# A two-layer GraphSAGE kernel: node aggregates kept in SBUF instead of a table of scanned rows in DRAM

## The chip, the cores and the metric

The kernel runs on one core of a Trainium2 chip. The metric is the device time of one execution in microseconds (us); smaller is better. Engines are named as in the profile: PE is TensorE (PEld its weight loads), DVE is VectorE, ACT is ScalarE, POOL is GpSimd, SP is SyncE, which here only issues DMAs.

## What is computed

12500 nodes with 128 features, 200000 edges (`src`, `dst`, a weight each), sorted by `dst`. Cut to what matters:

```python
h0   = relu(layernorm(x))
w    = edge_weight / max(segment_sum(edge_weight, dst), EPS)[dst]
feat = relu(h0 @ W_pool + b_pool)
neigh = segment_max(feat[src] * w[:, None], dst)        # 0 for a node without edges
rst  = h0 @ W1_self + neigh @ W1_neigh + b1
h    = relu(rst / max(norm(rst, axis=1), EPS))
neigh2 = segment_sum(h[src] * w[:, None], dst) / max(deg, 1)[:, None]
out  = x + relu(h @ W2_self + neigh2 @ W2_neigh + b2)
```

Each layer needs one row of 512 bytes for each edge, picked by `src`: 200000 rows gathered from a table in DRAM, twice.

## The kernel before

Nodes are cut into 98 tiles of 128, edges into 391 groups of 512 (390 whole ones, and one of 320). A group has four chunks of 128 edges. The program has five stages that follow each other, since each needs a table that the one before it leaves in DRAM.

**Prologue.** SP loads x (L114). For each node tile DVE works out mean and variance (L118, L119) and the normalized rows (L129); PE transposes them (L131), ACT takes the relu into `hT` (L132). PE multiplies with W_pool (L135) and adds the bias by a second matmul with one row (L136); DVE takes the relu `fr` (L138); SP stores it to the table `feat_d` (L139). Then the edge lists are loaded (L158 to L174), one group to a partition, and turned by PE transposes (L201) and DVE copies (L202) into columns: `srcT`, `ewT` and the high and low parts of `dst`. A number `unsorted`, worked out on the way, would send the kernel down a general path; with the inputs here it isn't taken.

**Edge phase**, once for each layer (`edge_phase`, L204). For each group POOL issues four indirect DMAs (L220), each of 128 rows of the table into `gt` (six buffers). ACT multiplies each chunk by the weights of its edges into `gs` (L225), PE transposes the chunks to `pm`, [feature, edge] (L227). PE spreads the row of segment starts over all partitions by a matmul with `pick` (L230), and ACT turns it into `keep` (L232). DVE runs one scan along the 512 edges (L235): a running max in layer 1, a running sum in layer 2, starting anew where `dst` changes, and carrying over from group to group. PE transposes the result back (`pr`, L243), ACT copies it to `rows` (L245), and SP stores the 256 KB to a table `scan_d` of 200000 rows (L246). In layer 1 DVE also makes one-hot tiles `a` and `b` (L254 to L259), from which PE sums each node's degree and weights (`hist`, L262).

**Node phase**, once for each layer. After layer 1's edges the degrees give the row of each node's last edge. For each four tiles POOL gathers those rows from `scan_d` (L305), DVE scales them (L309), PE transposes (L313), ACT copies (L315), and PE adds up the two products and the bias (L321 to L323). Layer 1 then divides by the norm (L365 to L372) and stores `h_d`, the second layer's table (L375); layer 2 adds x and stores the output (L396, L398).

The order on each engine is worked out by a scheduler from the program's order and its dependences; pools of buffers decide how far one engine may run ahead of another.

Of the kernel before, what the change touches and what calls it, by code (L numbers as in the profile page):

```python
# [16 lines left out]
P = 128  # L17
D = 128
G = 512          # edges of a group: one PSUM bank of fp32 columns
Q = 4            # chunks of 128 edges in a group; node tiles in a node group  # L20
NEG = -3.0e38    # below every message; added to the running maximum where a segment begins
LN_EPS = 1e-5
TINY = 1e-12     # EPS of the reference
PAST = 1 << 20   # a destination past every node, behind the last edge
SLOW_B = 64      # edges of one turn of the general path
# [3 lines left out]
def gnn_kernel(ctx, tc, x, src, dst, ew, w_pool, b_pool, w1s, w1n, b1, w2s, w2n, b2, out):  # L29
    """x + GraphSAGE(relu(layernorm(x))): a max-pooled layer and a mean layer over weighted edges.  # L30

    Edges are taken in order, in groups of 512. A group's source rows are gathered, weighted and
    transposed to [feature, edge]; one scan along the edges, restarted wherever dst changes, leaves
    each node's max (sum) at its last edge. The scanned rows go to a table in DRAM, and each node
    then fetches the row of its last edge. The edges come sorted by dst; a flag worked out on the
    chip says whether they are, and for edges in any other order a general path, one edge at a
    time, takes the scan's place.

    Node n = 128 * hi + lo lies on partition lo, column hi, of all per-node scalars.
    """  # L40
# [3 lines left out]
    HI = -(-N // P)                  # node tiles  # L44
    NP = HI * P                      # nodes, padded
    NF = N // P                      # whole node tiles
    GF, TAIL = divmod(E, G)          # whole groups, edges of the last one
    NG = GF + (TAIL > 0)
    NT = -(-NG // P)                 # blocks of 128 groups
    assert TAIL % Q == 0 and E % SLOW_B == 0 and E >= NP and D == x.shape[1]  # L50

    const = ctx.enter_context(tc.tile_pool(name="const", bufs=1))
    dram = ctx.enter_context(tc.tile_pool(name="dram", bufs=1, space=DRAM))
# [3 lines left out]
    scan1_d = dram.tile([E, D], F32, name="scan1_d")  # L57
    scan2_d = dram.tile([E, D], F32, name="scan2_d")

# [6 lines left out]
    for name, b in (("pool", b_pool), ("1", b1), ("2", b2)):  # L66
        Bv[name] = const.tile([1, D], F32, name=f"b_{name}")
        nc.scalar.dma_start(Bv[name], b[None, :])
    bp_col = const.tile([P, 1], F32)
    nc.scalar.dma_start(bp_col, b_pool[:, None])  # L70

    diff = const.tile([P, P], F32)      # column - partition
    nc.gpsimd.iota(diff, pattern=[[1, P]], base=0, channel_multiplier=-1,
                   allow_small_or_imprecise_dtypes=True)
    iota = const.tile([P, P], F32)      # column
    nc.gpsimd.iota(iota, pattern=[[1, P]], base=0, channel_multiplier=0,
                   allow_small_or_imprecise_dtypes=True)
    ident = const.tile([P, P], F32)
    nc.vector.tensor_scalar(ident, diff, 0.0, None, op0=OP.is_equal)
    upto = const.tile([P, P], F32)      # 1 where partition <= column  # L80
    nc.vector.tensor_scalar(upto, diff, 0.0, None, op0=OP.is_ge)
    ones = const.tile([P, P], F32)
    nc.vector.memset(ones, 1.0)

    hT = const.tile([P, HI, P], F32)    # layer inputs, [feature, node]
    begins = const.tile([P, NT, G], BF16)
    srcT = const.tile([P, NT, Q, P], I32)
    ewT = const.tile([P, NT, Q, P], F32)
    last = const.tile([P, HI], I32)     # row of each node's last edge
    s1 = const.tile([P, HI], F32)  # L90
    s2 = const.tile([P, HI], F32)
# [335 lines left out]
```

## Time and profile before

| | us |
|---|---|
| three runs of the kernel: median (lowest to highest) | 5526.82 (5515.38 to 5533.27) |
| span of the profiled execution, first to last instruction | 5500.3 |
| prologue, to the first gather of layer 1 | 0 to 262.8 |
| edge phase of layer 1 | 262.8 to 2703 |
| node phase of layer 1 | 2703 to 2944 |
| edge phase of layer 2 | 2944 to 5287 |
| node phase of layer 2 | 5287 to 5500 |

The profiled execution's own time isn't listed apart from its span; the median of the runs is 26.5 us above the span. A profile row such as `L220 POOL DMA_INDIRECT gt<-feat_d,srcT x1563 | 1564.4, 1001 | ...` gives the line of the program, the engine, the operation, what is written and read, how many there were, their busy time in us, the mean of one in ns, and then the engine's idle time just before them with what ended it. "issue" there means that the engine waited for nothing the profile could name. In a timeline row the first number is the start in us, the second the duration in us, and the idle time before stands in brackets. In a table of windows each engine's busy time stands with its number of instructions; behind them the granted TensorE clock (1 is full speed), the share of time in which DMA engines were busy, and GB/s.

### The profile page before, as it was taken

Reading aid. Unit: us, or ns where it says so; the run is one execution under the profiler, and the core shown is the slowest. Engines: PE = TensorE matmul, PEld = TensorE weight load, DVE = VectorE, ACT = ScalarE, POOL = GpSimd, SP = SyncE. Lnnn points to the kernel's source line nnn. Section 1 sums busy time; section 2 is a strip of 40 time slices with the busy share of each in tenths; the row PEclk is TensorE's granted clock in tenths of the full one; section 3 lists DMA queues with packets and bytes.
Section 4 is the critical chain, followed back from the end, with each engine's and each line's share of the span. In section 5 each row is a group of like instructions: output and inputs, shape, how many; then the busy total and the mean of one; then the engine's idle time right before and its main releaser. Section 6 shows DMA issues by size and latency. Waiting matters only on the chain. (4 is left out here: it accounts for less than half of the span.)

```text
span 5500.3 us, 41184 instructions
## 1 busy us (share of the span) xinstructions
PE 2928.3 (53%) x12192; PEld 2278.5 (41%) x12192; DVE 1829.8 (33%) x2502; ACT 1856.7 (34%) x4842; POOL 3234.2 (59%) x3328
## 2 busy tenths in 40 slices
PE   7645555565555555555585444444444444444459
PEld 4435554555545544555463223222222222222237
DVE  3334444444444444444422222222222222222211
ACT  0023333333333333333222333333333333333320
POOL 0066666666666666666444666666666666666653
PEclk9977777777777777777765555555555555555556
DMA  2122222222222222222221222223232222223233
GB/s 74 41 72 86 86 87 87 86 85 86 86 86 83 86 84 86 85 85 87 71 63 53 87 87 91 87 89 91 86 90 89 90 87 88 89 86 91 88 89 94
DMA packets 285584, 460.21 MB, mean 84 GB/s; under 512 B 67796, under 2 KB 131030, under 8 KB 285352
## 3 DMA queue, kind: packets, MB, share of 16 engines
q0 software_dynamic: 106304, 217.86, 15.4%
q1 hardware_dynamic: 178178, 239.30, 12.5%
q8 instruction: 100, 1.64, 0.1%
q14 instruction: 132, 1.08, 0.1%
q10 hardware_dynamic: 870, 0.33, 0.0%
HBM read 233.18 MB, written 224.05 MB: 83 GB/s over the span
## 5 line engine op out<-in xcount | busy, mean ns | idle before, releaser
L220 POOL DMA_INDIRECT gt<-feat_d,srcT x1563 | 1564.4, 1001 | 1105.8 <-issue 435.9
L220 POOL DMA_INDIRECT gt<-h_d,srcT x1563 | 1482.0, 948 | 905.4 <-issue 545.0
L235 DVE TENSOR_TENSOR_SCAN sc<-keep,sc,pm 128x512 f32<-128x512 f32 x780 | 997.3, 1279 | 2541.4 <-remote 1113.3
L243 PE MATMUL pr<-ident,sc 128*128 128x128 f32 x3128 | 786.5, 396 | 1557.5 <-DVE sc L235 977.6
L245 ACT ACTIVATE rows<-pr 128x512 f32<-128x512 f32 (+1 forms) x782 | 466.9, 597 | 2755.4 <-issue 2023.7
L243 PEld LDWEIGHTS pr<-ident,sc 128*128 128x128 f32 x3128 | 536.6, 216 | 1753.7 <-DVE sc L235 1065.4
L227 PE MATMUL pm<-ident,gs 128*128 128x128 f32 x3126 | 866.8, 372 | 346.4 <-ACT gs L225 240.0
L227 PEld LDWEIGHTS pm<-ident,gs 128*128 128x128 f32 x3126 | 574.5, 190 | 1113.5 <-ACT gs L225 519.4
L225 ACT ACTIVATE gs<-gt,ewT 128x128 f32<-128x128 f32 x3126 | 993.7, 393 | 118.1 <-DMA gt<-feat_d,srcT 75.0
L262 PE MATMUL hist<-a,b 128*128 128x196 f32 x3126 | 755.4, 397 | 0.0
L262 PEld LDWEIGHTS hist<-a,b 128*128 128x128 f32 x3126 | 708.9, 241 | 31.3 <-issue 0.2
L230 PE MATMUL pb<-begins,pick 128*128 128x512 bf16 (+1 forms) x782 | 419.8, 538 | 499.2 <-ACT rows L245 256.7
L232 ACT ACTIVATE keep<-pb 128x512 f32<-128x512 f32 (+1 forms) x782 | 462.4, 592 | 181.8 <-remote 139.3
L254 DVE TENSOR_TENSOR a<-hiT,iota 128x392 f32<-128x392 f32 x391 | 218.3, 558 | 558.8 <-remote 329.2
L305 POOL DMA_INDIRECT ng<-scan_d,last x196 | 187.1, 955 | 212.8 <-issue 52.7
L258 DVE TENSOR_TENSOR b<-loT,iota 128x512 f32<-128x512 f32 x391 | 268.9, 688 | 0.0
L256 DVE TENSOR_TENSOR a<-a,ewT 128x392 f32<-128x392 f32 x391 | 218.4, 558 | 0.0
L323 PE MATMUL po<-b,ones 1*128 1x128 f32 x392 | 130.6, 424 | 9.3 <-issue 9.3
L230 PEld LDWEIGHTS <-pick 128*128 128x128 bf16 x782 | 103.9, 133 | 16.4 <-issue 16.2
L315 ACT ACTIVATE nT<-pt 128x512 f32<-128x512 f32 (+1 forms) x50 | 28.7, 591 | 223.2 <-PE pt L313 164.8
L323 PEld LDWEIGHTS po<-b,ones 1*128 1x128 f32 x392 | 81.6, 257 | 45.4 <-issue 35.9
L135 PE MATMUL pf<-w_pool,hT 128*128 128x128 f32 x196 | 77.8, 501 | 9.0 <-ACT hT L132 9.0
(88 smaller groups left out, 1059.3 us busy)
## 6 DMA issues: line engine op xcount, KB each, us to landing
scan_d<-rows SPq DMA_DIRECT2D x780, 256.0 KB
gt<-feat_d,srcT POOLq DMA_INDIRECT x1563
gt<-h_d,srcT POOLq DMA_INDIRECT x1563
feat_d<-fr SPq DMA_DIRECT2D x24, 256.0 KB
h_d<-h SPq DMA_DIRECT2D x24, 256.0 KB
xr<-in_x SPq DMA_DIRECT2D x24, 256.0 KB
out<-o SPq DMA_DIRECT2D x24, 256.0 KB
xs<-in_x SPq DMA_DIRECT2D x6, 896.0 KB
```

Of the source, the lines that this page charges most:

```text
L220: nc.gpsimd.indirect_dma_start(out=gt[:k, j, :], out_offset=None, in_=table_d[:, :], in_offset=bass.IndirectOffsetOnAxis(ap=srcT[:k, t, j, ...
L225: nc.scalar.activation(gs[:k, j, :], gt[:k, j, :], AF.Copy, scale=ewT[:k, t, j, r:r + 1])
L227: nc.tensor.transpose(pm[:, j * P:j * P + k], gs[:k, j, :], ident[:k, :k])
L230: nc.tensor.matmul(pb[:, :ne], pick[:, r, :], begins[:, t, :ne], start=True, stop=True)
L232: nc.scalar.activation(keep[:, :ne], pb[:, :ne], AF.Copy, bias=0.0 if is_max else 1.0, scale=NEG if is_max else -1.0)
L235: nc.vector.tensor_tensor_scan(sc[:, :ne], keep[:, :ne], pm[:, :ne], carry, op0=OP.add if is_max else OP.mult, op1=OP.max if is_max else O ...
L243: nc.tensor.transpose(pr[:m, k, :], sc[:, k:ne:Q], ident)
L245: nc.scalar.activation(rows[:m], pr[:m], AF.Copy)
L254: nc.vector.tensor_tensor(a[:, :nj, 0, :], hiT[:, t, :nj, r:r + 1].to_broadcast([P, nj, HI]), iq[:, :, :HI].to_broadcast([P, nj, HI]), OP. ...
L256: nc.vector.tensor_tensor(a[:, :nj, 1, :], a[:, :nj, 0, :], ewT[:, t, :nj, r:r + 1].to_broadcast([P, nj, HI]), OP.mult)
L258: nc.vector.tensor_tensor(b[:, :nj, :], loT[:, t, :nj, r:r + 1].to_broadcast([P, nj, P]), iq.to_broadcast([P, nj, P]), OP.is_equal)
L262: nc.tensor.matmul(hist_psum, b[:k, j, :], a[:k, j], start=g == 0 and j == 0, stop=g == NG - 1 and j == nj - 1)
```

## The change

The tables `scan1_d` and `scan2_d` are gone, and with them `fetch` and the node phases as stages of their own. Aggregates lie in SBUF as `agg`, [feature, node], and a group of 512 edges touches 64 nodes at most, counted from the group's first `dst` (`bases`, one number a group, read into a register).

- **Prologue.** Edge lists are loaded ahead of x. The pool's bias is added by DVE (L180), and ACT takes the relu (L183). Degrees and sums of weights are worked out for every edge, ahead of the loops, by scans forward and backward along the groups (`node_sums`, L259), so that `w1T` is the layer-1 weight of each edge and `w2T` the layer-2 weight, with the degree in it. Rows that say where a segment begins go to a small table `keep_d` (L210). POOL clears `agg` (L186).
- **Layer 1.** Gathers (L312, eight buffers), scaling (L370), transposes (L371), scan (L373) and transposes back (L384, L386) stay. The row of segment starts is now spread by a DMA from `keep_d` (`kt`, 128 KB, L366). DVE compares each edge's node number with 64 columns (`sel`, L378), which is one only at a segment's last edge, and PE multiplies: `pa` = rows by `sel`, summed over the four chunks (L389, one PSUM buffer). ACT reads the group's base into a register (L391) and copies `pa` into its 64 columns of `agg` (L392). `pick`, `pb`, `keep`, `a`, `b` and `hist` are gone.
- **Layer 2.** No scaling on ACT, no transposes, no scan and no store: DVE makes a weighted one-hot tile `s` of 128 x 64 for each chunk (L406), PE sums gt by `s` (L410, three PSUM buffers), DVE reads the base (L412) and adds `pa` to its columns of `agg` (L413).
- **Node tiles** are worked on inside the loops, one tile about every four groups, four groups behind the edges (`due`, L317; `nodes1`, L328; `nodes2`, L346). `h_d` is stored a tile at a time.

The core of the diff (the body of the general path and the prologue's bookkeeping are left out):

```diff
-            for j in range(nj):
-                    k = min(P, ne - j * P)
-                    nc.gpsimd.indirect_dma_start(
-                        out=gt[:k, j, :], out_offset=None, in_=table_d[:, :],
...
-                pb = ps.tile([P, G], F32)
-                nc.tensor.matmul(pb[:, :ne], pick[:, r, :], begins[:, t, :ne], start=True, stop=True)
-                nc.scalar.activation(keep[:, :ne], pb[:, :ne], AF.Copy, bias=0.0 if is_max else 1.0,
-                                     scale=NEG if is_max else -1.0)
...
-                nc.sync.dma_start(
-                    scan_d[g * G:g * G + ne, :].rearrange("(p q) d -> p q d", q=Q), rows[:m])
...
+    with tc.tile_pool(name="eg", bufs=8) as gp, tc.tile_pool(name="ew", bufs=3) as wk, \
+            tc.tile_pool(name="ep", bufs=2, space=PSUM) as ps:
+        carry = NEG
+        for g in range(NG):
+            t, r, ne, chunks = edges_of(g)
+            gt = gather(gp, feat_d, g)
+            kt = wk.tile([P, G], BF16, bufs=6)
+            nc.sync.dma_start(kt[:, :ne], keep_d[g:g + 1, :ne].to_broadcast([P, ne]))
...
+            for j, k in chunks:
+                nc.scalar.activation(gs[:k, j, :], gt[:k, j, :], AF.Copy, scale=w1T[:k, t, j, r:r + 1])
+                nc.tensor.transpose(pm[:, j * P:j * P + k], gs[:k, j, :], ident[:k, :k])
+            sc = wk.tile([P, G], F32)
+            nc.vector.tensor_tensor_scan(sc[:, :ne], kt[:, :ne], pm[:, :ne], carry,
+                                         op0=OP.add, op1=OP.max)
...
+            nc.vector.tensor_tensor(
+                sel[:, :nj, :], iota[:, 1:2, :].to_broadcast([P, nj, LW]),
+                lastT[:, t, :nj, r:r + 1].to_broadcast([P, nj, LW]), OP.is_equal)
...
+                put = nc.scalar.activation(rows[:k, j, :], pr[:k, j, :], AF.Copy)
+            pa = ps.tile([P, LW], F32, bufs=1)
+            for j, k in chunks:
+                nc.tensor.matmul(pa, rows[:k, j, :], sel[:k, j, :], start=j == 0, stop=j == nj - 1)
+            with tc.issue_after(put.ins):
+                at = nc.scalar.value_load(bases[0:1, g:g + 1], min_val=0, max_val=N - 1)
+            nc.scalar.activation(agg[:, bass.ds(at, LW)], pa, AF.Copy)
+            for n in due(g):
+                nodes1(wk, ps, n, agg[:, n * P:(n + 1) * P], True)
+                nc.vector.memset(agg[:, n * P:(n + 1) * P], 0.0)
...
+            gt = gather(gp, h_d, g)
+            s = wk.tile([P, Q, LW], F32)
+            pa = ps.tile([P, LW], F32)
+            for j, k in chunks:
+                put = nc.vector.tensor_scalar(
+                    s[:k, j, :], iota[:k, 0, :], locT[:k, t, j, r:r + 1],
+                                        w2T[:k, t, j, r:r + 1], op0=OP.is_equal, op1=OP.mult)
+            for j, k in chunks:
+                nc.tensor.matmul(pa, gt[:k, j, :], s[:k, j, :], start=j == 0, stop=j == len(chunks) - 1)
+            with tc.issue_after(put.ins):
+                at = nc.vector.value_load(bases[0:1, g:g + 1], min_val=0, max_val=N - 1)
+            nc.vector.tensor_tensor(agg[:, bass.ds(at, LW)], pa, agg[:, bass.ds(at, LW)], OP.add)
+            for n in due(g):
+                nodes2(wk, ps, n, agg[:, n * P:(n + 1) * P])
```

ACT's queue in the middle of layer 1, before. `rows` is the transposed scan on its way to the store, `keep` the segment starts, `gs` the weighted rows.

```order
L245 ACTIVATE rows<-pr 128x512 [waits DMAHW7_49,PE_49,Activation_49]
L232 ACTIVATE keep<-pb 128x512 [waits DVE_49,PE_49]
L225 ACTIVATE gs<-gt,ewT 128x128 [waits DMASW0_49,Activation_49]
L225 ACTIVATE gs<-gt,ewT 128x128 [waits DMASW1_49]
L225 ACTIVATE gs<-gt,ewT 128x128 [waits DMASW2_49]
L225 ACTIVATE gs<-gt,ewT 128x128 [waits DMASW3_49]
```

The same place after, for two groups. TENSOR_LOAD and ISA are the reading of the base into a register, `agg<-pa` the copy into the aggregate's 64 columns.

```order
L386 ACTIVATE rows<-pr 128x512 [waits PE_49]
L391 TENSOR_LOAD bases
L391 ISA x2
L370 ACTIVATE gs<-gt,w1T 128x128 [waits DMASW2_49]
L392 ISA
L392 ACTIVATE agg<-pa 128x64 [waits PE_49,Activation_49]
L370 ACTIVATE gs<-gt,w1T 128x128 [waits DMASW3_49]
L370 ACTIVATE gs<-gt,w1T 128x128 [waits DMASW4_49,Activation_49]
L386 ACTIVATE rows<-pr 128x512 [waits PE_49]
```

`rows` no longer waits for a store, `keep` is gone, and a second instruction of the group waits for PE; one to three `gs` of later groups stand between the two.

PE's queue in layer 2, before: the transposes there and back, and the spreading of segment starts.

```order
L230 LDWEIGHTS pick
L230 MATMUL pb<-begins,pick 128x512 [waits Activation_49]
L227 MATMUL pm<-ident,gs 128x128 [waits PE_49,Activation_49]
L227 MATMUL pm<-ident,gs 128x128 [waits Activation_49]
L243 MATMUL pr<-ident,sc 128x128 [waits DVE_49]
L243 MATMUL pr<-ident,sc 128x128 x3
L227 MATMUL pm<-ident,gs 128x128 [waits Activation_49] x2
```

After, the same engine in layer 2: the gathered rows go straight into the sum, with the products of a due node tile (`pn`) between.

```order
L410 MATMUL pa<-s,gt 128x64 [waits DMASW2_49,DVE_49]
L410 MATMUL pa<-s,gt 128x64 [waits DMASW3_49,DVE_49]
L325 MATMUL pn<-w_2n,agg 128x128 [waits DVE_49]
L326 MATMUL pn<-b_79,ones 128x128
L410 MATMUL pa<-s,gt 128x64 [waits DMASW4_49]
L410 MATMUL pa<-s,gt 128x64 [waits DMASW5_49]
L324 MATMUL pn<-w_2s,hT 128x128 [waits DVE_49]
```

What was a chain of gather, ACT, PE, DVE, PE, ACT and SP is now gather and DVE, PE, DVE.

576 lines of the change are left out of this document (316 added, 260 removed).

## The prediction, made before the changed kernel had run

> **What bounds the kernel now.** I read the windows by stage first, because the span has stages of unlike limits: columns are the span of the window, busy us and instructions of PE, PEld, DVE, ACT and POOL, the granted clock, the DMA share and GB/s.
>
> ```profile
> 0.00:262.00 262.00, 185.70 (x555) 125.86 (x556) 93.46 (x353) 16.28 (x27) 0.63 (x6) 0.98 0.22 60
> 720.00:2600.00 1880.00, 1055.57 (x5188) 955.04 (x5187) 878.20 (x1220) 702.73 (x1830) 1215.48 (x1221) 0.77 0.29 86
> 2703.00:2975.00 272.00, 196.97 (x808) 153.59 (x809) 70.81 (x139) 55.66 (x122) 119.23 (x117) 0.62 0.19 53
> 3200.00:5200.00 2000.00, 888.91 (x3049) 561.78 (x3049) 433.83 (x339) 758.09 (x2029) 1269.81 (x1346) 0.51 0.29 89
> 5287.00:5500.00 213.00, 171.98 (x686) 133.56 (x686) 33.41 (x51) 14.38 (x25) 93.34 (x98) 0.63 0.33 92
> ```
>
> In the prologue and the node phases PE is the busy one. In the two edge phases none is busy all the time; POOL is nearest with 65%. Then the groups of the page that make up an edge phase, with what ended their waits:
>
> ```profile
> L220 POOL DMA_INDIRECT gt<-feat_d,srcT x1563 | 1564.4, 1001 | 1105.8 <-issue 435.9
> L220 POOL DMA_INDIRECT gt<-h_d,srcT x1563 | 1482.0, 948 | 905.4 <-issue 545.0
> L235 DVE TENSOR_TENSOR_SCAN sc<-keep,sc,pm 128x512 f32<-128x512 f32 x780 | 997.3, 1279 | 2541.4 <-remote 1113.3
> L243 PE MATMUL pr<-ident,sc 128*128 128x128 f32 x3128 | 786.5, 396 | 1557.5 <-DVE sc L235 977.6
> L245 ACT ACTIVATE rows<-pr 128x512 f32<-128x512 f32 (+1 forms) x782 | 466.9, 597 | 2755.4 <-issue 2023.7
> L227 PE MATMUL pm<-ident,gs 128*128 128x128 f32 x3126 | 866.8, 372 | 346.4 <-ACT gs L225 240.0
> L225 ACT ACTIVATE gs<-gt,ewT 128x128 f32<-128x128 f32 x3126 | 993.7, 393 | 118.1 <-DMA gt<-feat_d,srcT 75.0
> L262 PE MATMUL hist<-a,b 128*128 128x196 f32 x3126 | 755.4, 397 | 0.0
> L232 ACT ACTIVATE keep<-pb 128x512 f32<-128x512 f32 (+1 forms) x782 | 462.4, 592 | 181.8 <-remote 139.3
> ```
>
> A gather costs POOL 0.94 us and 0.30 us until the next, so 1.25 us, whenever nothing is in its way; the timeline of the middle of layer 1 shows that, and how it then stops:
>
> ```profile
> 1489.12 1.28 DVE L235 TENSOR_TENSOR_SCAN sc<-keep,sc,pm 128x512 f32<-128x512 f32 x1 [2.00 <-issue]
> 1490.45 0.75 PE L243 MATMUL pr<-ident,sc 128*128 128x128 f32 x4 [2.08 <-issue]
> 1495.76 0.94 POOL L220 DMA_INDIRECT gt<-feat_d,srcT  x1 [0.30 <-issue]
> 1497.00 0.95 POOL L220 DMA_INDIRECT gt<-feat_d,srcT  x1 [0.30 <-issue]
> 1497.77 0.60 ACT L245 ACTIVATE rows<-pr 128x512 f32<-128x512 f32 x1 [7.53 <-issue]
> 1501.88 1.16 POOL L220 DMA_INDIRECT gt<-feat_d,srcT  x1 [2.69 <-ACT gs L225]
> ```
>
> PE's transposes stand at 1490.45 to 1491.2, yet ACT gets on with them at 1497.77. ACT's queue is in order, so its `gs` wait too, the six `gt` buffers fill, and POOL stops. So POOL and a hesitating PE-ACT hand-over share the bound. A layer's gathers begin and end here:
>
> ```profile
> 262.77 9.16 POOL L220 DMA_INDIRECT gt<-feat_d,srcT  x1 [261.50 <-PE pt L201]
> 2670.57 0.91 POOL L220 DMA_INDIRECT gt<-feat_d,srcT  x1 [0.30 <-issue]
> 2943.97 8.44 POOL L220 DMA_INDIRECT gt<-h_d,srcT  x1 [63.73 <-issue]
> 5266.78 0.90 POOL L220 DMA_INDIRECT gt<-h_d,srcT  x1 [0.30 <-issue]
> ```
>
> Layer 1: (2671.5 - 262.8) / 1563 = 1.541 us a gather, 6.16 us a group. Layer 2: (5267.7 - 2944.0) / 1563 = 1.487, 5.95 us a group. POOL alone would be 4 x 1.25 = 5.0. Once the gathers of layer 1 are all issued, ACT takes a group every 3.3 us, without one long wait, and layer 2's end looks the same:
>
> ```profile
> 2683.49 0.60 ACT L245 ACTIVATE rows<-pr 128x512 f32<-128x512 f32 x1 [1.05 <-issue]
> 2686.78 0.60 ACT L245 ACTIVATE rows<-pr 128x512 f32<-128x512 f32 x1 [1.05 <-issue]
> 5285.99 0.59 ACT L245 ACTIVATE rows<-pr 80x512 f32<-80x512 f32 x1 [1.86 <-PEq L384]
> ```
>
> So the engines can do 3.3 us a group; the hesitation comes only while gathers stream. Its cause the trace doesn't name. The Trainium skill (SBUF — State Buffer, section "SBUF: two separate sides") says that engines and DMAs reach SBUF by separate ports, so that no transfer slows a compute instruction; this trace doesn't settle it, since what is late is PE's result and not the recorded length of its instructions.
>
> **The change, part by part.** *Prologue.* The rows:
>
> ```profile
> L129 DVE TENSOR_SCALAR xn<-xs,mv,rstd 128x128 f32<-128x128 f32 x98 | 28.3, 341 | 0.8
> L138 DVE TENSOR_SCALAR fr<-pf 128x512 f32<-128x512 f32 x24 | 16.6, 692 | 134.6 <-PE pf L136 134.6
> L136 PE MATMUL pf<-b_pool,ones 1*128 1x128 f32 x196 | 77.6, 497 | 0.0
> L176 DVE TENSOR_TENSOR begins<-dr 128x2048 bf16<-128x2048 int32 x1 | 2.3, 2281 | 0.0
> L197 DVE CAST rowf<-sr 128x2048 f32<-128x2048 int32 x1 | 1.2, 1227 | 18.2 <-DMA er<-in_edge_weight 18.2
> L123 DVE RECIPROCAL rstd<-rstd 128x98 f32<-128x98 f32 x1 | 0.8, 766 | 0.4 <-ACT rstd L122 0.4
> L370 DVE RECIPROCAL ss<-ss 128x4 f32<-128x4 f32 x24 | 4.2, 176 | 15.7 <-ACT ss L369 14.4 <-issue 0.8
> L202 DVE COPY loT<-pt 128x512 f32<-128x512 f32 x4 | 2.8, 692 | 1.3 <-PE pt L201 1.3
> ```
>
> Gone: the 196 bias records of L136, 77.6 us of the PE that sets the pace there. Added on DVE: 32 scans of 128 x 512 at 1.28 (41 us); two reciprocals of 128 x 2048, which by the step from 4 to 98 elements (590 / 94 = 6.3 ns an element) come to 13 us each; some ten two-input and three reducing operations at 2.3 (30); five or six one-input ones at 1.2 (7); 20 column copies at 0.69 (14) instead of 16; small ones 5. That is about 123 us. DVE's 93 us of the old prologue held some 23 us of edge lists (16 copies, three operations at 2.3, four at 1.2), so 70 for the norm stay, and PE's work falls from 186 to about 110 us, under DVE's 70 + 123 = 193. DVE is now the bound, and POOL's first gather comes behind nearly all of it. Ahead of it go some 20 us in which the lists load before x (the 18.2 of the cast's row), and I put 43 us on hand-overs with PE, a third of the 134.6 that `fr` waited for PE: first gather at 256. Bounds are 213 (no hand-over shown) and 363 (262.8 - 23 + 123, with nothing given back by PE). Against 262.8 that is hardly a change.
>
> *Layer 1's loop.* Gone from each group: `keep` on ACT (0.59), `a`, `b`, `a`, `pb` and eight `hist` records, 256 KB of store. Added: on PE four `pa` (a record of 128x128 costs 0.37 to 0.40), on ACT a register load and `agg` (under the 0.39 of a `gs`, since 64 columns are half as many), on DVE `sel` (256 elements), on SP 128 KB of `kt`. The register load I price by the one that each engine did for the flag:
>
> ```profile
> L356 ACTq TENSOR_LOAD <-unsorted x1: 468/468/468, 2702.6 to 2702.6; - x1
> ```
>
> So ACT has 4 x 0.39 + 0.60 + 0.47 + 0.39 + a quarter of a node tile's three instructions (under 0.4) = 3.4 us a group where it had 2.75, still far under 5.0. All of that lies beside the gathers. What decides is whether the hesitation stays. The chain that shows it (gs, pm, scan, pr, rows) stays whole, and layer 2 of before shows that it lasts without `hist`: 5.95 against 6.16. The bounds are 5.0 (gone) and 8.3 (a rival, below); nearest is the present row, with the same table and scan, so I keep 1.541: 1563 x 1.541 = 2409 us.
>
> One rule speaks for a small gain: 1001 ns a gather in layer 1 against 948 in layer 2, where DVE runs no a, b, a. The Trainium skill (SBUF — State Buffer, same section) says that GpSimd, which writes the descriptors, is locked out of SBUF while VectorE holds the port that they share. The first gather of either layer (9.16 and 8.44 us above) lies beside this row's copy, and agrees:
>
> ```profile
> 2942.90 8.69 DVE L210 CAST pick<-ident 128x16384 bf16<-128x16384 f32 x1 [2.19 <-DMA h_d<-h]
> ```
>
> The two copies of `pick` go. By the 53 ns, 1563 gathers would give back 83 us if POOL alone bound layer 1; here its stops would take that up, so the sum has nothing for it.
>
> *Layer 1 to 2.* The node phase (2703 to 2944, 241 us) goes into the loop, at a node tile a four groups. What is left is the drain: up to eight gathered groups at 3.3 us (26) and the last tiles with their store and the wait for it, about 16 (25 rounds of up to four tiles took 241 us there, under 10 us each). 42 us where there were 272 from the last gather to the first; between 20 and 60.
>
> *Layer 2's loop.* ACT, both sets of transposes, the scan and the store are gone. DVE makes four `s` (128x64, below the 0.34 of `xn`), loads a register and adds: under 2.7 us a group. PE has four matmuls instead of nine records; no ACT is between. A late PE result now holds up only DVE's `agg`, and `gt` is freed by PE itself. I take POOL's own pace: 1563 x 1.25 = 1954 us, between 1954 and the present 1.487 (2324).
>
> *End.* The node phase of 213 us and the 20 us drain ahead of it become the last group's sum and a tile or two with their store: 18 us (10 to 30).
>
> Sum: 256 + 2409 + 42 + 1954 + 18 = 4679 of span, against 5500.3. The median of the runs is 26.5 above the span: **4706 us**.
>
> **The rivals.**
> 1. *POOL bounds both layers.* The hesitation goes in layer 1 too, as `pb`, `hist` and the stores have gone. 256 + 1954 + 20 + 1954 + 18 + 26.5 = 4229. Against it: layer 2 of before has neither `hist` nor much of DVE and hesitates still. The Trainium skill's rule of separate ports (SBUF — State Buffer, section "SBUF: two separate sides") would make the streaming itself harmless to PE, and so speaks for this one; the 3.3 us groups that begin when gathers end speak against the rule's use here.
> 2. *Layer 2 hesitates as before.* If PE is late because of the streaming alone, four matmuls are late like nine, and POOL stops on `gt` all the same: 4706 + 370 = 5076.
> 3. *Slower: layer 1 runs one group after another.* ACT waits for PE twice a group now, for `rows` and for `agg`, `pa` has one buffer, and what is queued behind `agg` is the next groups' `gs`. If each hand-over is late, a group costs its whole chain: four gs 1.57, pm 0.37, scan 1.28, four pr 0.75, rows 0.60, four pa 0.75, agg 0.39, and one hesitation of 7.5 us for each two groups, 9.5 us: 256 + 391 x 9.5 + 42 + 1954 + 18 + 26.5 = 6011. It decides from 8.3 us a group ((5527 - 2297) / 391), or from 7.3 if rival 2 holds as well. For it: PE's lateness hits exactly such waits. Against it: with one such wait a group `rows` loses 2.6 us a group today (2023.7 / 782, below), while POOL loses less than half of that, and one to three `gs` of later groups stand between the two waits.
>
> ```profile
> ACT rows L245 <- issue: 2023.7, 558, 12.3
> POOL gt L220 <- ACT gs L225: 752.3, 217, 8.1
> ```
>
> 4. *The change doesn't do what it says*: the limits on the groups' nodes fail and the general path runs, edge by edge. With 32 nodes a group on average and room for 64 I give it next to nothing.
>
> **How the numbers follow.** Forecast 0.43; rival 1 0.21; rival 2 0.27; rival 3 0.06; between the two paces of layer 1, 0.03. An even result would need rival 3 to stop just at 8.3 us: 0.01 (within 0.3% is about what a measurement here can tell from no change). Faster: 0.94, slower 0.05. For 8 in 10 the range must reach rivals 1 and 2: with rival 1's bound, less 9, and rival 2's, plus 44 of prologue and drain, 4220 to 5120. The forecast's own range is 4640 to 4830, by the bounds of the prologue (-43, +107), the drain and the end.
>
> **What would show it.** In the profile after: the first gather near 256 us; in layer 1 `rows` still with waits of 5 us and more, and POOL stopped by ACT's `gs`, at 6.2 us a group; in layer 2 POOL with 0.30 before each gather throughout, and 5.0 us a group; some 40 us from the last gather of layer 1 to the first of layer 2. The forecast is wrong if layer 1 has no such waits (rival 1), if POOL stops in layer 2, its releaser being PE (rival 2), or if `agg` on ACT heads the waits with more than 7 us a group (rival 3).

## The result and the profile after

The changed kernel takes 5294.58 us (median of four runs, 5290.59 to 5301.02) against 5526.3 (5515.38 to 5533.27) beside it: a ratio of 0.9587, 95% interval 0.957 to 0.9605. The forecast was 4706 us, its range 4220 to 5120: the way was right, the size was not, and the time lies above the range. The profiled execution took 5301.02 us, its span is 5299.2; so only 1.8 us lie outside the span, not 26.5.

The windows of the changed kernel, cut where its stages part:

```profile
0.00:229.00 229.00, 79.58 (x393) 64.34 (x394) 187.41 (x440) 31.77 (x58) 12.06 (x16) 0.70 0.24 71
229.00:2988.00 2759.00, 1677.71 (x6786) 1363.93 (x6786) 709.19 (x1145) 869.96 (x2679) 1477.99 (x1563) 0.51 0.23 58
2988.00:3032.00 44.00, 37.77 (x159) 31.55 (x158) 16.00 (x34) 17.95 (x61) 0.10 (x1) 0.54 0.06 15
3032.00:5279.00 2247.00, 909.49 (x3662) 815.43 (x3661) 510.12 (x2029) 0.00 (x0) 1478.22 (x1563) 0.50 0.20 52
5279.00:5299.00 20.00, 12.73 (x49) 10.82 (x48) 4.88 (x20) 0.00 (x0) 0.12 (x1) 0.50 0.05 14
```

and the first and last gather of either layer in its timeline:

```profile
228.91 1.11 POOL L312 DMA_INDIRECT gt<-feat_d,srcT  x1 [103.15 <-DVE w2T L195]
2987.19 0.91 POOL L312 DMA_INDIRECT gt<-feat_d,srcT  x1 [0.30 <-issue]
3032.03 0.96 POOL L312 DMA_INDIRECT gt<-h_d,srcT  x1 [43.93 <-issue]
5278.21 0.91 POOL L312 DMA_INDIRECT gt<-h_d,srcT  x1 [0.30 <-issue]
```

The node phases are gone as forecast, all but 44 and 20 us. But layer 1's loop has become slower than it was: (2988.1 - 228.9) / 1563 = 1.765 us a gather, 7.06 us a group, where it was 6.16. Layer 2 takes 1.438 a gather, 5.75 a group, where it was 5.95 and where POOL alone would take 5.0.

The groups and the waits show that PE's late hand-over has stayed in both layers, and whom it now holds up:

```profile
L312 POOL DMA_INDIRECT gt<-feat_d,srcT x1563 | 1478.2, 946 | 1384.2 <-ACT gs L370 789.7
L312 POOL DMA_INDIRECT gt<-h_d,srcT x1563 | 1478.3, 946 | 812.7 <-issue 479.8
L413 DVE TENSOR_TENSOR agg<-pa,agg 128x64 f32 x391 | 87.9, 225 | 1426.0 <-remote 1077.5
L392 ACT ACTIVATE agg<-pa 128x64 f32 x391 | 88.3, 226 | 1079.5 <-remote 686.3
```

```profile
DVE agg L413 <- remote: 1077.5, 142, 19.9
PE pa L410 <- DVE s L406: 401.9, 71, 12.1
POOL gt L312 <- ACT gs L370: 789.7, 106, 9.2
ACT agg L392 <- remote: 686.3, 115, 26.3
POOL gt L312 <- remote: 224.6, 89, 8.6
```

"remote" means that the profile found no instruction or DMA behind the wait's end; that it is PE's result follows from the kernel, since `agg` waits for `pa` alone. One case of layer 2, from its timeline. Counted in order, the sum that DVE takes up at 4210.54 is of products that PE had recorded by 4193.9, in the first of these rows (the eight records of 4200.39 belong to the sum that it takes up two later, at 4213.38). DVE was free from 4201.1. POOL, whose buffer PE must free, stops for 3.9 us and goes on 0.24 us after DVE; the next `s` stands behind `agg` in DVE's queue, so PE too waits, until 4211.63.

```profile
4191.71 3.94 PE L410 MATMUL pa<-s,gt 128*128 128x64 f32 x18
4200.39 1.97 PE L410 MATMUL pa<-s,gt 128*128 128x64 f32 x8 [4.74 <-issue]
4205.92 0.95 POOL L312 DMA_INDIRECT gt<-h_d,srcT  x1 [0.30 <-issue]
4210.54 0.23 DVE L413 TENSOR_TENSOR agg<-pa,agg 128x64 f32 x1 [9.45 <-remote]
4210.78 0.95 POOL L312 DMA_INDIRECT gt<-h_d,srcT  x1 [3.91 <-remote]
4211.63 0.69 PE L410 MATMUL pa<-s,gt 128*128 128x64 f32 x2 [9.27 <-DVE s L406]
```

The same count over all 391 sums of layer 2 gives the lateness a size: from the recorded end of a sum's last product, or of DVE's instruction before if that is later, `agg` starts 3.3 us late on the mean, over 1 us in 202 of 391 cases, up to 19.9 us.

In layer 1 ACT now meets the late hand-over at both of its instructions that wait for PE, here twice within 6 us:

```profile
1516.38 0.23 ACT L392 ACTIVATE agg<-pa 128x64 f32 x1 [7.03 <-remote]
1521.94 0.60 ACT L386 ACTIVATE rows<-pr 128x512 f32<-128x512 f32 x1 [4.76 <-remote]
```

A gather itself is now 946 ns in layer 1 as in layer 2, where it was 1001 and 948: with `a`, `b`, `a` gone from DVE, POOL's busy time falls by 86 us, about the 83 of the prediction (8 of them are the first gather, 9.16 us beside the copy of `pick`, now 1.11). The trace of the kernel before shows where the rest was: of its 290 gathers above 0.98 us in layer 1, 281 overlap L256, where DVE multiplied `a` by the weights. The end time keeps none of it, since POOL stops for longer than that.

### The profile page after: what moved, and what is told of

Its sections match the earlier page's. It is cut to its first block, busy times and chain, and to the rows that moved or that the text cites. A ratio compares the mean times of both kernels' runs of the same rounds, so it can differ in the third digit from the quotient of the medians.

```text
span 5299.2 us, 39480 instructions
## 1 busy us (share of the span) xinstructions
PE 2717.3 (51%) x11044; PEld 2286.1 (43%) x11044; DVE 1427.6 (27%) x3665; ACT 919.7 (17%) x2797; POOL 2968.5 (56%) x3141
## 4 chain that ended last, share of the span: by engine, by line
another core or an unknown queue 35%; PE 32%; issue 15%; DVE 12%; ACT 3%; DVEq 1%; DMA 1%; ACTq 0%; POOL 0%; SPq 0%; POOLq 0%
PE pa L410 9%; PE pa L389 7%; DVE sc L373 6%; PE pr L384 5%; PE pm L371 3%; DVE s L406 3%; PE pn L325 2%; PE pn L326 2%; PE pn L324 2%; ACT gs L370 1%; ACT rows L386 1%; DVE agg L413 1%; DVEq L412 1%; PE pf L178 1%
## 5 line engine op out<-in xcount | busy, mean ns | idle before, releaser
L312 POOL DMA_INDIRECT gt<-feat_d,srcT x1563 | 1478.2, 946 | 1384.2 <-ACT gs L370 789.7
L312 POOL DMA_INDIRECT gt<-h_d,srcT x1563 | 1478.3, 946 | 812.7 <-issue 479.8
L410 PE MATMUL pa<-s,gt 128*128 128x64 f32 x3126 | 734.9, 422 | 563.0 <-DVE s L406 401.9
L410 PEld LDWEIGHTS pa<-s,gt 128*128 128x128 f32 x3126 | 695.2, 330 | 608.1 <-DVE s L406 416.1
L389 PE MATMUL pa<-sel,rows 128*128 128x64 f32 x3126 | 745.2, 419 | 236.0 <-issue 184.7
L389 PEld LDWEIGHTS pa<-sel,rows 128*128 128x128 f32 x3126 | 691.5, 325 | 343.6 <-issue 251.8
L373 DVE TENSOR_TENSOR_SCAN sc<-kt,sc,pm 128x512 f32<-128x512 bf16 x390 | 498.6, 1279 | 512.6 <-PE pm L371 304.3
L384 PE MATMUL pr<-ident,sc 128*128 128x128 f32 x1563 | 415.5, 419 | 298.3 <-DVE ss L335 241.0
L370 ACT ACTIVATE gs<-gt,w1T 128x128 f32<-128x128 f32 x1563 | 539.8, 395 | 142.5 <-DMA gt<-feat_d,srcT 108.5
L371 PE MATMUL pm<-ident,gs 128*128 128x128 f32 x1563 | 487.7, 429 | 100.0 <-ACT gs L370 69.6
L413 DVE TENSOR_TENSOR agg<-pa,agg 128x64 f32 x391 | 87.9, 225 | 1426.0 <-remote 1077.5
L406 DVE TENSOR_SCALAR s<-iota,locT,w2T 128x64 f32<-128x64 f32 x1563 | 437.3, 340 | 84.8 <-issue 82.9
L384 PEld LDWEIGHTS pr<-ident,sc 128*128 128x128 f32 x1563 | 303.0, 231 | 342.5 <-DVE ss L335 256.2
L378 DVE TENSOR_TENSOR sel<-iota,lastT 128x256 f32<-128x256 f32 x391 | 165.1, 423 | 1010.0 <-remote 549.1
L371 PEld LDWEIGHTS pm<-ident,gs 128*128 128x128 f32 x1563 | 311.8, 211 | 205.6 <-ACT gs L370 113.4
L386 ACT ACTIVATE rows<-pr 128x512 f32<-128x512 f32 (+1 forms) x393 | 233.5, 595 | 490.1 <-remote 234.9
L392 ACT ACTIVATE agg<-pa 128x64 f32 x391 | 88.3, 226 | 1079.5 <-remote 686.3
```

What stands on the lines that cost most here:

```text
L312: nc.gpsimd.indirect_dma_start(out=gt[:k, j, :], out_offset=None, in_=table_d[:, :], in_offset=bass.IndirectOffsetOnAxis(ap=srcT[:k, t, j, ...
L370: nc.scalar.activation(gs[:k, j, :], gt[:k, j, :], AF.Copy, scale=w1T[:k, t, j, r:r + 1])
L371: nc.tensor.transpose(pm[:, j * P:j * P + k], gs[:k, j, :], ident[:k, :k])
L373: nc.vector.tensor_tensor_scan(sc[:, :ne], kt[:, :ne], pm[:, :ne], carry, op0=OP.add, op1=OP.max)
L378: nc.vector.tensor_tensor(sel[:, :nj, :], iota[:, 1:2, :].to_broadcast([P, nj, LW]), lastT[:, t, :nj, r:r + 1].to_broadcast([P, nj, LW]), ...
L384: nc.tensor.transpose(pr[:k, j, :], sc[:, j * P:j * P + k], ident)
```

## The experiments

Theory A: under the stream of gathers PE's results come late by an amount that grows with PE's own work. Theory B: ACT's waits for PE in layer 1 cost it its 0.9 us a group. Theory C: each hand-over from PE is late by itself. D (the lateness belongs to some chips), E (it needs indirect gathers) and F (any stream of loads does it) came later and stand in the texts.

The runs fell on several chips, and these are of two kinds, which has to be known to read any number below. On two, and on that of the first runs, which may be one of the two, the kernel before takes about 5530 us (5536; 5512 to 5543 in seven runs). On four others it takes 4655 to 4669. I call them the first and the second kind; times are compared on one chip only, unless the text says otherwise. One chip was seen at two times (4655 and 4669 us), and none in both kinds; that the kind belongs to the chip, and not to the moment, is likely but not shown.

**e1_few_gathers** (second kind). The rows of eight groups are gathered once and used again, so most messages are those of the wrong edges.

```diff
+        if g >= 8:
+            return kept[g % 8]
-        gt = pool.tile([P, Q, D], F32, name="gt")
+        gt = kept[g] = pool.tile([P, Q, D], F32, name="gt")
```

> The changed kernel with only the first eight groups of each layer gathered; the later groups use those eight tiles again, so most messages are those of the wrong edges. Theory A (PE delivers late only while gathers stream, by an amount that grows with its own work): without the stream layer 1 takes 3.3 to 4.3 us a group and layer 2 2.3 to 3, some 2900 us in all. Theory B (the order of waits on ACT in layer 1 serialises the groups, whatever POOL does): layer 1 stays near 7.06 us a group, layer 2 falls; 4200 us and more in all.

It took 3094.72 us. Windows of the two loops:

```profile
270.00:1900.00 1630.00, 1519.11 (x6787) 1276.01 (x6787) 720.30 (x1146) 857.32 (x2675) 0.00 (x0) 0.60 0.14 35
1990.00:3070.00 1080.00, 894.87 (x3488) 784.78 (x3488) 478.68 (x1927) 0.00 (x0) 0.00 (x0) 0.50 0.04 12
```

Without a stream PE is busy 93% of layer 1; from layer 1's first gather at 229.3 to layer 2's at 1919.8 and on to the end at 3092.8 a group takes 4.3 us and 3.0. So the order of the waits doesn't by itself serialise layer 1, and both loops have room under POOL's 5.0. What a stream does to PE the run can't say: on this very chip PE's results aren't late with a full stream either (e3 to e5, next).

**e3_one_sum, e4_sums_twice, e5_agg_dve** (the same chip, second kind), and their repeats **f3_one_sum, f4_sums_twice, f5_agg_dve** (another of the second kind). The first makes `pa` from one chunk of four, the second makes it twice over, the third copies `pa` on DVE to columns that are counted by the group's number, not by its nodes, in layer 1.

```diff
# e3, in both layers
-            for j, k in chunks:
+            for j, k in chunks[:1]:
# e4, in both layers
-            for j, k in chunks:
+            for i, (j, k) in enumerate(chunks + chunks):
# e5
-            with tc.issue_after(put.ins):
-                at = nc.scalar.value_load(bases[0:1, g:g + 1], min_val=0, max_val=N - 1)
-            nc.scalar.activation(agg[:, bass.ds(at, LW)], pa, AF.Copy)
+            nc.vector.tensor_copy(agg[:, g * 32:g * 32 + LW], pa)
```

> The changed kernel with one of the four products that make pa, in both layers (three quarters of each group's sums are left out); all waits between engines stay. Theory A: PE's recorded work falls by some 1.4 us a group in both layers; with two thirds of a us of time for each recorded us of PE work layer 1 goes from 7.06 to about 6.1 us a group and layer 2 from 5.75 to about 5.0. Theory B: the two waits of ACT stay, layer 1 stays within 0.2 of 7.06. Theory C (the streaming delays each hand-over by itself, whatever PE has to do): both layers stay within 0.2.

> The changed kernel with the four products that make pa done twice, the second time over the first (same result). PE's recorded work grows by some 1.9 us a group, to 6.2 in layer 1 and 4.2 in layer 2. Theory A: layer 1 about 8.3 us a group, layer 2 about 7.0, about 6300 us in all. Theories B and C: the products lengthen one hand-over by 1 us at most and PE was recorded busy under 62%, so layer 1 stays under 7.6 and layer 2 within 0.3 of 5.75.

> The changed kernel with layer 1's copy of pa into agg on DVE instead of ACT, to columns counted by the group's number and without the register load (aggregates then lie in columns that are not their nodes'). ACT waits for PE only once a group, as before the change. Theory A: layer 1 stays within 0.3 of 7.06 us a group. Theory B: layer 1 falls to 6.2 or less, the pace of the kernel before.

> Once more the changed kernel with one of the four products that make pa, in both layers (three quarters of each group's sums are left out), in the hope of a chip on which the kernel before takes about 5530 us. There Theory A (PE is late under indirect gathers by an amount that grows with its own work): layer 1 about 6.1 us a group instead of 7.0, layer 2 about 5.0 instead of 5.75, some 4640 us in all. Theory C (each hand-over is late by itself, whatever PE has to do): 5270 us within 100. On a chip where the kernel before takes near 4670 nothing is told apart: 4157 again.

> Once more the changed kernel with the products that make pa done twice. On a chip where the kernel before takes about 5530 us: Theory A: layer 1 about 8.3 us a group, layer 2 about 7.0, some 6250 us in all. Theory C: 5270 us within 150. On a chip where the kernel before takes near 4670: 4170 again.

> Once more the changed kernel with layer 1's copy of pa into agg on DVE, to columns counted by the group's number (aggregates then lie in columns that are not their nodes'); ACT waits for PE once a group. On a chip where the kernel before takes about 5530 us: Theory A: layer 1 stays at 6.9 to 7.2 us a group, 5270 us within 100 in all. Theory B (ACT's second wait costs layer 1 its 0.9 us a group): layer 1 6.2 us, some 4930 us in all. On a chip where the kernel before takes near 4670: 4153 again.

They took 4157.06, 4169.79 and 4152.7 us beside a kernel before of 4668.28, and 4155.16, 4167.0 and 4157.42 beside 4655.27. No theory had foreseen that: each layer keeps POOL's pace in all three edits. The two loops of e4, the one with most work:

```profile
227.00:2178.00 1951.00, 1760.63 (x9984) 1600.05 (x9985) 726.12 (x1159) 901.01 (x2716) 1474.85 (x1563) 0.71 0.34 83
2204.00:4155.00 1951.00, 1665.86 (x6815) 1519.81 (x6815) 525.96 (x2045) 0.00 (x0) 1474.78 (x1563) 0.50 0.23 60
```

1951 / 1563 = 1.248 us a gather in both, though PE is busy 90% and 85%. DVE's waits for PE in layer 2 are 3.2 us on the mean and 6.6 us at most:

```profile
DVE agg L414 <- PE pa L411: 1253.5, 391, 6.6
```

These are waits for products still being made: by the count above, `agg` starts 0.04 us late in layer 2 of e3, e4, e5, f5 and e8, 0.1 us at most in 391 sums each. So on a chip of this kind POOL's 4 x 1.248 = 4.99 us a group is the bound with room to spare, and these six runs tell A, B and C apart no further.

**e6_changed_again** (first kind): the changed kernel, unaltered.

> The changed kernel itself, unaltered, beside the kernel before, once more. On the chip of the four runs ahead of this one the kernel before took 4668 us where it took 5526 beside the changed kernel's first runs, and all four kept POOL's own pace of 1.248 us a gather. Theory D (PE's late results under streaming gathers belong to some chips only): on a chip where the kernel before takes near 4670 the changed kernel takes 4150 to 4175, and on one where it takes near 5526, 5295 again; nothing between. Theory A', that the lateness depends on the program alone: 5295 wherever it runs.

5273.05 us beside 5535.99, and `agg` of layer 2 starts 3.3 us late on the mean again: as theory D has it.

**e2_plain_loads** (the same chip, first kind). Each indirect gather becomes a load by SP of 128 rows that lie together; POOL issues nothing in the loops.

```diff
-            nc.gpsimd.indirect_dma_start(
-                out=gt[:k, j, :], out_offset=None, in_=table_d[:, :],
-                in_offset=bass.IndirectOffsetOnAxis(ap=srcT[:k, t, j, r:r + 1], axis=0))
+            o = (g * Q + j) % HI * P
+            nc.sync.dma_start(gt[:k, j, :], table_d[o:o + k, :])
```

> The changed kernel with each indirect gather replaced by SP's plain load of 128 rows that lie together (messages are then those of the wrong edges); POOL issues nothing in the loops. On a chip where PE's results come late: Theory E (it is the indirect gathers, descriptors written by POOL, that go with the lateness): both layers lose their long waits, layer 1 takes 3.5 to 4.5 us a group, layer 2 2.5 to 3.5, some 3000 us in all. Theory F (any stream of 64 KB loads into SBUF does it): long waits stay, over 5 us a group in both. On a chip without late results both give the first figure, unless SP's four issues a group cost more.

3250.21 us. The windows of the loops, and the heads of the list of waits:

```profile
224.00:2255.00 2031.00, 1768.42 (x6930) 1389.46 (x6930) 745.82 (x1168) 877.46 (x2731) 0.00 (x0) 0.50 0.29 80
2255.00:3241.00 986.00, 923.63 (x3719) 837.55 (x3719) 511.77 (x2057) 1.70 (x8) 0.00 (x0) 0.50 0.42 117
```

```profile
DVE sel L377 <- PE pa L388: 641.3, 388, 3.9
ACT agg L391 <- PE pa L388: 630.4, 379, 1.7
```

As many bytes go to the same tiles, on a chip of the first kind, and at 117 GB/s in layer 2 faster than gathers ever brought them; yet no wait at the head of the list is longer than 3.9 us, PE is busy 87% and 94%, and a group takes 5.2 and 2.5 us. `agg` of layer 2 starts 0.04 us late, 0.1 us at most, where it was 3.3 on the same chip in e6. So it is the indirect gathers that POOL issues that go with the lateness (theory E), not loads into SBUF as such (F falls). The edit changes who issues, how the rows are addressed and where they lie, all at once; which of these matters isn't told apart. Layer 1 is longer than E's 4.5: PE's records alone make 4.5 us a group there. The Trainium skill (SBUF — State Buffer, section "SBUF: two separate sides") says that DMAs and engines don't slow each other; this run agrees, with 117 GB/s of loads and no late result. What POOL's descriptors or its gathers do to PE on some chips, the page doesn't say.

**e9_l1_dve_l2_twice** (another chip of the first kind; its twin **e8_l1_dve_l2_twice** fell on the second kind, 4155.04 us beside 4657.98). Layer 1 as in e5, layer 2 as in e4.

> Two edits in one kernel, since the layers follow each other: in layer 1 the copy of pa into agg on DVE, to columns counted by the group's number (ACT waits for PE once a group; aggregates then lie in other columns), in layer 2 the products that make pa done twice. On a chip where the kernel before takes about 5530 us: Theory A (PE late under indirect gathers, by an amount that grows with its own work): layer 1 stays at 6.9 to 7.2 us a group, layer 2 goes from 5.75 to about 7.0. Theory B (ACT's second wait): layer 1 6.2. Theory C (each hand-over late by itself): layer 2 stays within 0.3 of 5.75. On a chip where the kernel before takes near 4660: 4.99 us a group in both.

> Once more two edits in one kernel: in layer 1 the copy of pa into agg on DVE, to columns counted by the group's number (ACT waits for PE once a group; aggregates then lie in other columns), in layer 2 the products that make pa done twice. On a chip where the kernel before takes about 5530 us: Theory A: layer 1 stays at 6.9 to 7.2 us a group, layer 2 goes from 5.75 to about 7.0. Theory B: layer 1 6.2. Theory C: layer 2 stays within 0.3 of 5.75. On a chip where the kernel before takes near 4660: 4155 again.

5066.24 us, where the changed kernel took 5270.99 on the same chip. Its first and last gathers, and the windows between:

```profile
224.79 1.11 POOL L312 DMA_INDIRECT gt<-feat_d,srcT  x1 [103.35 <-DVE w2T L195]
2731.18 0.90 POOL L312 DMA_INDIRECT gt<-feat_d,srcT  x1 [0.30 <-issue]
2767.26 0.96 POOL L312 DMA_INDIRECT gt<-h_d,srcT  x1 [35.17 <-issue]
5031.16 0.91 POOL L312 DMA_INDIRECT gt<-h_d,srcT  x1 [0.30 <-issue]
```

```profile
225.00:2732.00 2507.00, 1432.61 (x6777) 1264.55 (x6777) 748.05 (x1525) 739.01 (x2297) 1478.12 (x1563) 0.59 0.26 64
2768.00:5032.00 2264.00, 1551.59 (x6725) 1474.89 (x6725) 509.94 (x2022) 0.00 (x0) 1477.30 (x1563) 0.50 0.20 51
```

Layer 2: 2264.8 / 1563 = 1.449 us a gather with twice the products, 5.79 us a group against 5.75 (5.74 for the changed kernel on this chip): PE's busy time rises by 70%, the pace by nothing. Theory A falls; it would have had 7.0. C's forecast holds, though not each hand-over is late: `agg` starts over 1 us late in 214 of the 391 sums here and in 206 in the changed kernel on this chip. A timeline piece shows the same picture as with single products: the sum taken up at 4220.74 was recorded by 4213.2, and POOL stops just before it goes on.

```profile
4207.67 5.97 PE L409 MATMUL pa<-s,gt 128*128 128x64 f32 x27
4220.74 0.23 DVE L412 TENSOR_TENSOR agg<-pa,agg 128x64 f32 x1 [8.74 <-remote]
4220.98 0.95 POOL L312 DMA_INDIRECT gt<-h_d,srcT  x1 [1.28 <-remote]
```

Layer 1: 1.604 us a gather, 6.41 a group against 1.742 (6.96) for the changed kernel on this chip: 0.55 of the 0.8 by which that exceeds the kernel before (6.16, on the chip of the first runs) goes when `agg` leaves ACT, not all as B had it (6.2). The edit also drops the register load, fixes the columns and lets the scheduler place node tiles otherwise, and the granted clock is 0.59 instead of 0.51; so the 0.55 belong to the edit, and that they are ACT's second wait is the likeliest reading, not shown. The traces add a caution: adding up the waits of over 1 us past PE's last record, ACT stood on PE's results, at `rows` and `agg`, for 806 us in layer 1 of the kernel before, 921 after, 942 in the changed kernel on this chip and 1014 here, with one wait a group. The lateness itself hardly grew. What differs is how much of it reaches POOL: the layer's gathers took longer than 1563 x 1.248 = 1951 us by 458 (83 of them for longer gathers), 808, 772 and 556 us.

**e10_changed_timed** (the same chip, first kind): the changed kernel in three rounds.

> The changed kernel itself, timed in three rounds against the kernel before. On a chip where the kernel before takes near 4660 us and every variant so far kept POOL's pace: 4150 to 4165, a ratio of 0.892. On one where it takes about 5530: 0.957 again.

5270.99 us (5263.27 to 5277.41) beside 5527.91 (5512.14 to 5543.12), ratio 0.9542 (0.951 to 0.9574).

**e7_bf16_sums, f7_bf16_sums, g2_bf16_sums, g4_bf16_sums** (four times the second kind). The operands of the sums in bf16 (`rows` too), with a copy of `gt` made by ACT in layer 2.

```diff
-            sel = wk.tile([P, Q, LW], F32)
+            sel = wk.tile([P, Q, LW], BF16)
...
+            gb = wk.tile([P, Q, D], BF16)
+            for j, k in chunks:
+                nc.scalar.activation(gb[:k, j, :], gt[:k, j, :], AF.Copy)
```

> The changed kernel with the operands of the sums in bf16: layer 1's rows and sel, layer 2's s and a copy of gt that ACT makes, idle in layer 2 till now (sums are then those of rounded messages). A product is one record of PE instead of two, and a short one; the waits stay, with one more in layer 2. On a chip where the kernel before takes about 5530 us: Theory A: PE's work falls by at least 1 us a group, layer 1 to 6.2 us or less, layer 2 to 5.0 to 5.2, 4400 to 4700 us in all. Theory C: 5270 within 100 or more. On a chip where the kernel before takes near 4670: 4150 to 4180.

> Once more the changed kernel with the operands of the sums in bf16 (sums of rounded messages). On a chip where the kernel before takes about 5530 us: Theory A: layer 1 6.2 us a group or less, layer 2 5.0 to 5.2, 4400 to 4700 us in all. Theory C: 5270 within 100 or more. On a chip where the kernel before takes near 4660: 4160 again.

> Once more the changed kernel with the operands of the sums in bf16 (sums of rounded messages), half as many records of PE for them. On a chip where the kernel before takes about 5530 us: Theory A has fallen for more work; if it held for less, layer 1 would take 6.2 us and layer 2 5.0 to 5.2. Theory C: 6.9 to 7.1 and 5.6 to 5.9. On a chip where the kernel before takes near 4660: 4160 again.

> Once more the changed kernel with the operands of the sums in bf16 (sums of rounded messages), half as many records of PE for them. On a chip where the kernel before takes about 5530 us: Theory A, if it held for less work: layer 1 6.2 us a group, layer 2 5.0 to 5.2. Theory C: 6.9 to 7.1 and 5.6 to 5.9. On a chip where the kernel before takes near 4660: 4160 again.

4159.93, 4155.47, 4156.62 and 4159.69 us, beside 4655 to 4669: POOL's pace again. What it does on a chip of the first kind stays open.

**g1_no_nodes_l2_pause, g3_no_nodes_l2_pause** (both the second kind). Layer 1 as in e5 and without node tiles, so that layer 2 gathers the pooled features; in layer 2 POOL clears a tile after each four gathers.

```diff
             gt = gather(gp, h_d, g)
+            idle = wk.tile([P, G], F32)
+            nc.gpsimd.memset(idle, 0.0)
```

> In layer 1 the copy of pa into agg on DVE to columns counted by the group's number, and no node tiles at all (layer 2 then gathers the pooled features, stored twice, and its results are others); ACT waits for PE at rows alone. In layer 2 POOL clears a tile of 128x512 after each four gathers, some 0.48 us by the clearing of 128x2048 in 1.80. On a chip where the kernel before takes about 5530 us: Theory B (each wait of ACT on PE costs layer 1 some time): layer 1 falls from 6.41 us a group, with agg on DVE alone, to 6.16 or less. Theory C (late hand-overs cost the same however many ACT waits for): 6.3 to 6.5. Layer 2: if PE catches up in any pause of POOL, 5.5 us a group with few stops; if it needs the long ones, 5.75 or more, up to 6.2. On a chip where the kernel before takes near 4660: 4.99 and 5.5.

> Once more: in layer 1 the copy of pa into agg on DVE to columns counted by the group's number, and no node tiles at all (layer 2 then gathers the pooled features and its results are others); ACT waits for PE at rows alone. In layer 2 POOL clears a tile of 128x512 after each four gathers, which on a chip of the second kind made 5.37 us of a group. On a chip where the kernel before takes about 5530 us: Theory B: layer 1 6.16 us a group or less. Theory C: 6.3 to 6.5. Layer 2: if PE catches up in any pause of POOL, about 5.4 us a group with few stops; if it needs the long ones, 5.75 or more. On a chip where the kernel before takes near 4660: 4304 again.

4304.05 and 4306.46 us. First and last gather of layer 2 of g1:

```profile
2178.80 0.96 POOL L313 DMA_INDIRECT gt<-h_d,srcT  x1 [2.38 <-ACT gs L371]
4287.72 0.90 POOL L313 DMA_INDIRECT gt<-h_d,srcT  x1 [0.30 <-issue]
```

2109.8 / 391 = 5.40 us a group (5.37 stood in g3's text), 0.41 more than 4.99, for a clearing of 0.54 us that stands in place of one of the pauses of 0.30 between gathers. So what is added to POOL shows in the time, which confirms POOL as the bound on that kind. Whether such pauses let PE catch up on the first kind wasn't seen.

## Why the prediction was wrong

Term by term, in us of span: the first gather 228.9 (forecast 256); layer 1 2759 (2409); drain 44 (42); layer 2 2247 (1954); end 20 (18); outside the span 2 (26.5). The two loops make 643 too little, the rest 48 too much.

- **The step that failed first: layer 2, "I take POOL's own pace".** It rested on ACT being gone, on PE freeing `gt` by itself, and on "a late PE result now holds up only DVE's `agg`". But the stops were not ACT's doing. PE's results are late with one hand-over a group too (3.3 us on the mean), and that hand-over holds up more than `agg`: the next `s` stands behind it on DVE, so PE waits in its turn (401.9 us), and `gt`, which PE's own late result frees, comes late to POOL. e9 shows 5.79 us even with twice the products in PE, so its load doesn't set it. Rival 2 had this mechanism, with 0.27 and a price of 370 us; 293 came. The row that spoke for it stood in the prediction: PE's transposes recorded at 1490.45, taken up at 1497.77.
- **Layer 1, "so I keep 1.541".** The hesitation stayed, as forecast, but its size didn't: 7.06 us a group. I priced ACT's added instructions by their busy time, 3.4 us under POOL's 5.0, and so at nothing. That term had no wait in it: `agg`, and a node tile's `sq`, are two more places where ACT, in order, meets a late result. e9 gives back 0.55 by taking `agg` off ACT. The likeliest reading is rival 3's mechanism at about a quarter of its size, 0.9 us a group where its 9.5 would have been 3.3 more than 6.16: the stops are as long as before, but fewer are hidden from POOL. Which part of the edit does it stays open, and so do the other 0.25 to 0.35 us a group.
- **The range** left out rivals 2 and 3 together. I priced each alone, and gave the upper end as rival 2 plus 44 of prologue and drain: 5120. Both hang on one cause, PE's lateness, so they had to be added: with the 0.9 us a group that came on top of 5076 the sum is 5430, above the measured time. (The forecast's own range, 4640 to 4830, is also a little narrower than its bounds make it, 4633 to 4843; nothing hangs on that.)
- **Rival 1, POOL in both layers at 4229 us, is what chips of the second kind do, as far as variants tell.** The changed kernel itself wasn't run on one; e4, which has all its work and more, took 4169.79 beside 4668.28, a ratio of 0.893 from one run each. Had the four first runs fallen there, the forecast would very likely have been too high; that wasn't run. The kernel before takes about 870 us less there as well, so the chip moves the time more than the change does.
- **Right:** the prologue (DVE 187.41 busy against 193 forecast), the drains, the gathers' 53 ns and that no store or PE work bounds the loops. The 43 us of hand-overs ahead of the first gather were too many: 229 - 187 leaves 42 for them and the loading of the lists together.

What stays open: why PE hands over late on some chips while POOL's indirect gathers stream. It went with the gathers (e2), it didn't grow with PE's products (e9), and it wasn't on every chip. Nor is it known whether PE finishes late or its signal comes late, since the ends of PE's records are modelled. One trait of the record goes with it: the traces of the first kind with gathers hold 21276 to 24330 updates of semaphores, the signals that waits end on, where those of e2, with plain loads, and of e3 to e5, on the second kind, hold 71142 to 72245; this may be why the profile says "remote" and "issue" there, and whether it has one cause with the lateness isn't known. Whether fewer PE records, pauses in POOL or node tiles off ACT relieve it there was not seen, since those runs fell on the other kind. The granted clock in layer 1, 0.77 before and 0.51 after, may have its part in layer 1's 0.9 us; no run holds it fixed.

## What to carry to other kernels

A wait whose releaser the profile can't name ("issue", "remote") has no known cause, so removing an engine beside it removes nothing for sure: price the loop with the wait kept, and let every new instruction that waits for the late engine, on an engine with an ordered queue, cost time, however short it is. A timeline row shows when a record stands, not whose result it is: count the products through to their reader before calling a hand-over late. Rivals that share one cause are added, not taken one by one, when the range is drawn. Where a loop hangs on such a wait, take the kernel before along on every chip: here the pair of times is 5530 and 5270 on one kind; on the other it is about 4660 and, for variants of the changed kernel, 4150 to 4170.

## What the runs showed of the hardware

- One and the same program takes 16% less on some chips than on others: 5512 to 5543 us on two or three of them, 4655 to 4669 on four, with nothing between.
- On the first kind DVE and ACT wait up to 20 and 26 us at a time for PE's results while indirect gathers stream (the changed kernel), and 3.9 us at most at the head of the list while plain loads of the same size do, at up to 117 GB/s. DVE takes up layer 2's sums 3.3 us late on the mean with gathers (e6) and 0.04 us with plain loads (e2, the same chip), and 0.04 us with gathers on the second kind (e3, e4, e5).
- An indirect gather of 128 rows costs POOL 1.248 us when nothing stops it (0.946 and 0.30), the same in e3, e4, e5 and e7, though PE is busy 25% of layer 2 in the first (486.6 of 1950 us) and 90% of layer 1 in the second.
